# Top-p graph attention on one core: a 27-round search for the nucleus against a guess, two exact sums and 48 sorted candidates

## The chip, the cores and the metric

The kernel runs on one core of a Trainium2 chip. The core has five engines that run beside each other, each with its own queue of instructions that it takes strictly in order: TensorE (PE, with its weight loads PEld), VectorE (DVE), ScalarE (ACT), GpSimd (POOL) and SyncE (SP), which here only issues transfers. They wait for each other with semaphores. PE writes to PSUM; everything else lies in SBUF, 128 partitions wide. The metric is the device time of one execution in microseconds. All arithmetic is in float32.

## The reference

3,327 nodes with 256 features, an adjacency matrix `S` with about 0.12% of its entries set, and two steps of a graph layer. What matters:

```python
h = relu(layernorm(x))                         # X of what follows
def _top_p_attention(X, W1, W2, W3):
    q = X @ W1.T @ W2.T                        # 64 columns
    k = X @ W3.T
    probs = softmax(q @ k.T)                   # 3327 x 3327
    idx = argsort(-probs); sp = probs sorted
    keep_sorted = cumsum(sp) - sp < 0.9        # the nucleus of each row
    A = probs * mask
    return A / max(A.sum(-1), 1e-12)
R = (S + I) / rowsum
for n in range(2):
    A = _top_p_attention(Xa, W1, W2, W3)
    Xf = R @ Xf;  Xa = A @ Xa
    Z = Z + Xf @ U1[n].T + Xa @ U2[n].T
out = x + layernorm(X + Z) * g + b
```

Per row, the nucleus is the smallest set of the largest weights whose sum reaches 0.9 of the row's sum. Its size differs from row to row, and the reference finds it by sorting.

## The kernel before

The nodes are padded to 3,328 = 26 tiles of 128 rows. A tile's row of weights, 128 x 3,328, is a buffer `e`. Features (`x0`, `xf1`, `xa1`) and keys (`kT`) stay in SBUF for the whole run; only the adjacency, 1.7 MB per tile, comes from memory, once per step.

For each step the kernel first makes the keys of all tiles (L276), then works in groups of two tiles, 13 per step:

- `weights` (L124 to L145): queries, logits on PE in 512 columns each (L138), a copy from PSUM on ACT (L139), the row's maximum on DVE (L141), the exponential with its sum `z` on ACT (L143). It is called one group ahead.
- `diffuse` (L221 to L234): `R @ Xf` for the group's tiles on PE (L227), the input of the adjacency in two halves on SP.
- `nucleus` (L148 to L199): a binary search for the smallest weight of the nucleus, over the 27 low bits of a float, in place for both tiles of a group. Each round tries a candidate: ACT sums what lies over it (Relu, L165), DVE counts the weights that reach it (L168), and six DVE operations on two columns (L170 to L176, L162) turn the bit. After the rounds DVE zeroes what is smaller (L187), and treats weights equal to the threshold, of which only some belong to the nucleus, by a running count (L190, L192, L198, L199).
- `attend` (L202 to L216): transposes of `e` on PE (L208), copies of four at a time on ACT (L210), and `A @ Xa` on PE (L212), with the row's sum as column 257, whose reciprocal `ra` (L215) scales the result (L216).
- `finish` (L242 to L265), in the second step: the products with U1 and U2 (L253), a layernorm (L107 to L110, L261) and the output.

A scheduler orders each engine's instructions by their dependencies, so that a queue mixes instructions of neighbouring tiles: the work of attend and diffuse on PE and ACT lies beside the rounds of the next group. PE, with 30% of the span, waits most of the time.

In the listings, a name with a number is a buffer (`e_13582` is one tile's weights), and "waits" names the engine whose semaphore an instruction waits for.

## Time and profile before

| | |
|---|---|
| median of three runs | 7589.15 us (7588.61 to 7589.69) |
| profiled execution, span | 7591.1 us |
| instructions | 32,413 |
| busy: DVE, ACT, PE, POOL | 94%, 67%, 30%, 2% |
| transferred | 102.37 MB, mean 13 GB/s |

The profile is one execution; its own time is given by its span of 7591.1 us, the first to the last instruction, which is 2 us above the median of the runs. A row of a group reads: line, engine, operation, output<-inputs, size of the output and the input, count | total busy us, mean ns of one | idle time of the engine just before them and what ended it. A row of the timeline reads: start us, duration us, engine, line, operation. Matmuls come in float32 as two instructions for each matrix product of the code, so a tile's 26 blocks are 52 rows.

### The profile page before, as it was taken

The numbers are of one execution on the slowest core, as the hardware profiler recorded it, in microseconds if no ns is written. First come the engines' busy times: TensorE is split into PE (matmuls) and PEld (weight loads), VectorE is DVE, ScalarE is ACT, GpSimd is POOL, SyncE is SP. The second block draws the span as 40 slices with busy tenths as digits, with TensorE's granted clock in tenths as the row PEclk, the third lists the DMA queues.
The fourth block names the chain that finished last, engine by engine and source line by source line (L and its number), as shares of the span: only waits on it lengthen the run. The fifth ranks groups of instructions, "written<-read, shape, count | busy, mean of one in ns | idle before, by whom it ended". The sixth has DMA issues, their size and how long they took to land.

```text
span 7591.1 us, 32413 instructions
## 1 busy us (share of the span) xinstructions
PE 2264.7 (30%) x8840; PEld 1616.4 (21%) x8840; DVE 7155.3 (94%) x8060; ACT 5056.3 (67%) x4057; POOL 152.0 (2%) x295
## 2 busy tenths in 40 slices
PE   8783113113113113111324043043143142142222
PEld 5662102102102102101203032032032032132121
DVE  7999999999999999999789999999999999999997
ACT  6576676676676676676576766766766766766754
POOL 1000000000000000000000000000000000000000
PEclk9995555556556556555657576576576576576666
DMA  3230000000000000000000000000000000000000
GB/s 108 86 103 1 0 0 0 0 0 0 0 0 0 0 0 0 0 0 0 0 0 17 4 21 15 6 21 12 9 21 11 11 21 6 15 21 6 15 3 2
DMA packets 28071, 102.37 MB, mean 13 GB/s; under 512 B 3313, under 2 KB 14576, under 8 KB 27888
## 3 DMA queue, kind: packets, MB, share of 16 engines
q1 hardware_dynamic: 25888, 98.84, 4.0%
q10 hardware_dynamic: 2000, 1.46, 0.1%
q8 instruction: 70, 1.15, 0.1%
q14 instruction: 113, 0.93, 0.0%
HBM read 96.88 MB, written 3.41 MB: 13 GB/s over the span
## 4 chain that ended last, share of the span: by engine, by line
DVE 83%; ACT 7%; PE 6%; issue 4%; POOL 0%; DVEq 0%; DMA 0%; POOLq 0%; ACTq 0%
DVE jv L168 59%; ACT ja L165 5%; DVE nth L192 5%; PE pl L138 3%; DVE e L187 2%; DVE eq L198 2%; DVE e L199 2%; PE pr L227 2%; DVE low L172 2%; DVE cand L176 2%; DVE low L174 2%; DVE mass L171 1%; DVE ncand L162 1%; DVE mass L170 1%; ACT e L143 1%
## 5 line engine op out<-in xcount | busy, mean ns | idle before, releaser
L168 DVE TENSOR_SCALAR_CACHE_REDUCE jv<-e,cand 128x3328 uint8<-128x3328 f32 x1404 | 5161.3, 3676 | 36.6 <-ACT e L143 8.4
L165 ACT ACTIVATE ja<-e,ncand 128x3328 uint8<-128x3328 f32 x1404 | 4308.7, 3069 | 1197.8 <-DVE ncand L162 1173.3
L208 PE MATMUL pt<-ident,e 128*128 128x128 f32 x1352 | 208.9, 298 | 4770.2 <-DVE e L199 4770.2
L208 PEld LDWEIGHTS pt<-ident,e 128*128 128x128 f32 x1352 | 178.3, 154 | 4808.8 <-issue 4719.1
L210 ACT COPY eT<-pt 128x512 f32<-128x512 f32 (+1 forms) x364 | 189.5, 553 | 937.0 <-PE pt L208 936.7
L138 PE MATMUL pl<-kT,qT 64*128 64x512 f32 (+1 forms) x728 | 460.5, 778 | 77.3 <-ACT e L139 59.7
L212 PE MATMUL pa<-x,eT 128*128 128x257 f32 x1352 | 386.9, 446 | 152.7 <-ACT eT L210 82.5
L192 DVE TENSOR_TENSOR_SCAN nth<-eq 128x3328 int16<-128x3328 uint8 x52 | 368.6, 7088 | 0.9
L212 PE MATMUL pa<-xa,eT 128*128 128x257 f32 x1352 | 343.4, 407 | 47.5 <-ACT eT L210 47.5
L227 PE MATMUL pr<-x,at 128*128 128x257 f32 x1352 | 326.7, 400 | 77.3 <-issue 69.8
L227 PE MATMUL pr<-xf,at 128*128 128x256 f32 x1352 | 335.1, 396 | 29.3 <-DVE xf L233 25.0
L212 PEld LDWEIGHTS pa<-x,eT 128*128 128x128 f32 x1352 | 295.6, 226 | 225.0 <-ACT eT L210 101.2
L227 PEld LDWEIGHTS pr<-x,at 128*128 128x128 f32 x1352 | 265.9, 200 | 133.2 <-issue 83.7
L212 PEld LDWEIGHTS pa<-xa,eT 128*128 128x128 f32 x1352 | 266.5, 203 | 110.3 <-ACT eT L210 71.1
L227 PEld LDWEIGHTS pr<-xf,at 128*128 128x128 f32 x1352 | 256.4, 197 | 91.4 <-issue 31.6
L165 ACT ACTIVATION_READ_ACCUMULATOR ja<-e,ncand 128x1 f32 x1404 | 263.4, 188 | 0.0
L139 ACT COPY e<-pl 128x512 f32<-128x512 f32 (+1 forms) x364 | 188.0, 553 | 97.4 <-PE pl L138 97.4
L141 DVE TENSOR_REDUCE bias<-e 128x1 f32<-128x3327 f32 x52 | 187.9, 3613 | 52.9 <-ACT e L139 52.9
L138 PEld LDWEIGHTS pl<-kT,qT 64*128 64x128 f32 x728 | 161.1, 245 | 326.8 <-ACT e L139 201.9
L171 DVE TENSOR_TENSOR mass<-mass,over 128x2 f32<-128x2 f32 x702 | 113.6, 162 | 114.8 <-ACT ja L165 52.1
L198 DVE SCALAR_TENSOR_TENSOR eq<-nth,lim,eq 128x3328 uint8<-128x3328 int16 x52 | 191.8, 3689 | 1.8
L199 DVE SCALAR_TENSOR_TENSOR e<-eq,ncand,e 128x3328 f32<-128x3328 uint8 x52 | 191.6, 3685 | 1.9
(67 smaller groups left out, 2132.2 us busy)
## 6 DMA issues: line engine op xcount, KB each, us to landing
at<-in_adj SPq DMA_DIRECT2D x104, 832.0 KB, 4.4
xr<-in_x SPq DMA_DIRECT2D x26, 128.0 KB, 2.2
out<-y SPq DMA_DIRECT2D x25, 128.0 KB, 1.7
x<-in_x SPq DMA_DIRECT2D x6, 512.0 KB, 6.9
u<-in_u1t ACTq DMA_DIRECT2D x2, 256.0 KB, 5.7
u<-in_u2t ACTq DMA_DIRECT2D x2, 256.0 KB, 6.0
x<-in_x SPq DMA_DIRECT2D x1, 256.0 KB, 9.7
gam<-in_ln_g ACTq DMA_DIRECT2D x1, 128.0 KB, 5.1
```

What stands on the lines that cost most here:

```text
L138: nc.tensor.matmul(pl[:, :w], qT, kT[:, j : j + w], start=True, stop=True)
L139: nc.scalar.copy(e[:, j : j + w], pl[:, :w])
L165: nc.scalar.activation(ja, es[a], AF.Relu, bias=ncand[:, a : a + 1], accum_out=over[:, a : a + 1])
L168: nc.vector.tensor_scalar(jv, es[a], cand[:, a : a + 1], None, ALU.is_ge, ALU.add, accum_out=cnt[:, a : a + 1])
L171: nc.vector.tensor_tensor(mass, mass, over, ALU.add)
L192: nc.vector.tensor_tensor_scan(nth, eq, eq, 0.0, ALU.add, ALU.max)
L198: nc.vector.scalar_tensor_tensor(eq, nth, lim[:, c], eq, ALU.is_ge, ALU.mult)
L199: nc.vector.scalar_tensor_tensor(e, eq, ncand[:, c], e, ALU.mult, ALU.add)
L208: nc.tensor.transpose(pt[:, j, :], e[:, (j0 + j) * P : (j0 + j + 1) * P], ident)
L210: nc.scalar.copy(eT[:, :w, :], pt[:, :w, :])
L212: nc.tensor.matmul(pa, eT[:, j, :], xa[:, j0 + j, :], start=j0 + j == 0, stop=j0 + j == NT - 1)
L227: nc.tensor.matmul(pr[:, :w], at[:, j, :], xf[:, jj, :w], start=jj == 0, stop=jj == NT - 1)
```

## The change

The whole old layer stays, under the name `search_graph_layer`. A new `guess_graph_layer` does the layer with another search, and keeps a flag for every row whose answer cannot be vouched for. At the end PE adds up the flags, a register takes the sum, and a branch runs `search_graph_layer` as well if it is over zero.

The new search assumes that the logits of a row are roughly normal, so that weights are lognormal. The exponential is taken without the maximum, straight from PSUM (L477). From the row's sum and from the first two moments of its logits (which come out of one matmul with the mean and the second moments of the keys, `mq`) POOL computes by a fitted polynomial a threshold `c0` (column 9 of `g`), in about 27 operations on one column (`weights`). Then:

- `first`: ACT sums exactly what lies over `c0` (Relu, L520) and how many that are (Sign, L522). POOL makes a better threshold `c1` (column 13).
- `second`: DVE sums exactly what lies under `c1` (L536). POOL takes a secant step, adds a margin, and gets `c2` (column 16), meant to lie a little over the answer.
- `settle`: DVE zeroes everything from `c2` on (L571) and sums the rest; it finds the eight largest of each of 20 segments of 168 (L576), merges these 160 into the 48 largest in order (`ROUNDS` = 6, L581 and L583), adds them up from the largest down, compares with what is still needed, and zeroes in `e` what is smaller than the last candidate of the nucleus (L594). Its checks go to the flag (L599 to L605): that 48 were enough, that no segment had more than its eight, that no equal weights straddle the end, and that the sum lies in a range.
- `close`: `attend` as before, then `finish`, or in the first step `prep`, which makes the next step's keys, queries and moments. `spread` is the diffusion, with the adjacency in blocks of five tiles and three buffers.

The work goes tile by tile, not in groups, in a loop written in stages: in one turn settle of tile i, second of tile i+1, close of tile i-1, weights of tile i+3, first of tile i+2 and spread of tile i. Four buffers hold `e`. The keys lie in two halves of 64 partitions, so that two logit products of one turn stand on different rows of PE's array.

```diff
-        nucleus(es, z)
...
-            for i, t in enumerate(ts):
...
+        pq = ps_t.tile([P, 4, P], F32, tag="pt", name="pq")
+        PE.matmul(pq[:, 0, :], w2d[qp, :], qry[qp, j, :], start=True, stop=True)
+        PE.matmul(pq[:, 1:3, :].rearrange("p a b -> p (a b)")[:, : 2 * DA + 1], qry[qp, j, :],
+                  qm[qp, step, :], start=True, stop=True)
+        qT = tpool.tile([P, P], F32, tag="qT", name="qT", bufs=2)
+        S.copy(qT, pq[:, 0, :])
...
+        V.tensor_copy(mq[:, 0:1], pr_[:, 2 * DA : 2 * DA + 1])
+        qs = small.tile([P, DA], F32, tag="qs", name="qs", bufs=2)
+        V.tensor_copy(qs, pr_[:, :DA])
+        V.scalar_tensor_tensor(qj, qs, 1.0, pr_[:, DA : 2 * DA], ALU.mult, ALU.mult,
+                               accum_out=mq[:, 1:2])
+        G.memset(e[:, N:NP], 0.0)
...
+            if wd == 512:
+                S.activation(e.rearrange("p (a n) -> p a n", a=2)[:, :, c : c + wd], pl[:, :, :wd],
+                             AF.Exp, accum_out=za[:, n : n + 1])
...
+        G.tensor_tensor(g[:, 5:7], za[:, 0:2], za[:, 2:4], ALU.add)
+        G.tensor_tensor(col(0), col(5), col(6), ALU.add)
+        G.tensor_tensor(col(1), col(0), pwr[:, 5:6], ALU.pow)
+        G.tensor_scalar(col(1), col(1), 10.0, None, ALU.mult)
+        G.tensor_scalar(col(2), m, m, mq[:, 1:2], ALU.mult, ALU.subtract)
+        G.tensor_scalar(col(2), col(2), -1.0e-6, None, ALU.min)
+        G.tensor_scalar(col(3), col(2), -1.0, None, ALU.mult)
+        G.tensor_tensor(col(3), col(3), pwr[:, 3:4], ALU.pow)
+        G.tensor_scalar(col(5), col(2), -0.5, m, ALU.mult, ALU.add)
+        G.tensor_tensor(col(5), pwr[:, 1:2], col(5), ALU.pow)
+        G.tensor_scalar(col(5), col(5), col(0), 0.1 / N, ALU.mult, ALU.mult)
+        G.tensor_scalar(col(5), col(5), YLO, YHI, ALU.max, ALU.min)
+        G.tensor_tensor(col(4), col(5), pwr[:, 4:5], ALU.pow)
+        y = col(4)
+        G.tensor_scalar(col(6), y, PG[0], PG[1], ALU.mult, ALU.add)
+        for a in PG[2:]:
+            G.tensor_scalar(col(6), col(6), y, a, ALU.mult, ALU.add)
+        G.tensor_scalar(col(8), col(6), col(3), m, ALU.mult, ALU.add)
+        G.tensor_scalar(col(8), col(8), col(2), None, ALU.subtract)
+        G.tensor_tensor(col(9), pwr[:, 0:1], col(8), ALU.pow)
+        G.tensor_scalar(col(10), col(9), -1.0, None, ALU.mult)
+        G.tensor_scalar(col(7), y, -PK[0], -PK[1], ALU.mult, ALU.add)
+        G.tensor_scalar(col(7), col(7), y, -PK[2], ALU.mult, ALU.add)
+        G.tensor_scalar(col(11), col(7), col(3), None, ALU.mult)
...
+    def first(r):
+        e, col = r["e"], r["col"]
+        oa = small.tile([P, 2], F32, tag="oa", name="oa")
+        ja = scan.tile([P, NP], U8, tag="ja", name="ja")
+        S.activation(ja, e, AF.Relu, bias=col(10), accum_out=oa[:, 0:1])
+        ja = scan.tile([P, NP], U8, tag="ja", name="ja")
+        S.activation(ja, e, AF.Sign, bias=col(10), accum_out=oa[:, 1:2])
+        G.tensor_scalar(col(5), oa[:, 1:2], 0.5, NP / 2.0, ALU.mult, ALU.add)
+        G.tensor_scalar(col(5), col(5), col(9), oa[:, 0:1], ALU.mult, ALU.add)
+        G.tensor_scalar(col(5), col(5), col(0), col(1), ALU.subtract, ALU.mult)
+        G.tensor_scalar(col(12), col(5), -1.0, 0.1, ALU.mult, ALU.max)
+        G.tensor_scalar(col(5), col(12), 10.0, None, ALU.min)
+        G.tensor_tensor(col(5), col(5), col(11), ALU.pow)
+        G.tensor_scalar(col(13), col(5), col(9), None, ALU.mult)
+    def second(r):
+        e, col = r["e"], r["col"]
+        d1 = small.tile([P, 1], F32, tag="d1", name="d1")
+        jv = scan.tile([P, NP], F32, tag="w", name="jv")
+        V.scalar_tensor_tensor(jv, e, col(13), e, ALU.is_lt, ALU.mult, accum_out=d1)
+        r1, c1 = col(14), col(13)
+        G.tensor_scalar(r1, d1, col(1), 1.0e-6, ALU.mult, ALU.max)
...
+        G.tensor_tensor(col(6), col(6), col(5), ALU.pow)
+        G.tensor_scalar(col(6), col(6), c1, None, ALU.mult)
+        G.tensor_scalar(col(7), c1, 30.0, d1, ALU.mult, ALU.add)
+        G.tensor_scalar(col(7), col(7), col(0), BIG, ALU.is_gt, ALU.mult)
+        G.tensor_scalar(col(8), r1, 0.35, BIG, ALU.is_lt, ALU.mult)
+        G.tensor_scalar(col(16), col(6), col(7), col(8), ALU.add, ALU.add)
+    def settle(r, rows):
+        e, col = r["e"], r["col"]
+        d2 = small.tile([P, 1], F32, tag="d2", name="d2")
+        need = small.tile([P, 1], F32, tag="need", name="need")
+        w = scan.tile([P, NP], F32, tag="w", name="w")
+        V.scalar_tensor_tensor(w, e, col(16), e, ALU.is_lt, ALU.mult, accum_out=d2)
+        G.tensor_scalar(col(17), col(0), -0.1, None, ALU.mult)
+        G.tensor_tensor(need, d2, col(17), ALU.add)
+        cand = small.tile([P, NSEG * 8], F32, tag="cand", name="cand", bufs=1)
+        for s in range(NSEG):
+            V.max(cand[:, 8 * s : 8 * s + 8], w[:, s * SEG : min(NP, (s + 1) * SEG)])
+        v = small.tile([P, 4], F32, tag="v", name="v")
+        V.tensor_reduce(v[:, 0:1], cand.rearrange("p (s k) -> p s k", k=8)[:, :, 7], AX.X, ALU.max)
+        for k in range(ROUNDS):
+            b8 = bb[:, 1 + 8 * k : 9 + 8 * k]
+            V.max(b8, cand)
+            if k < ROUNDS - 1:
+                V.match_replace(cand, b8, cand, 0.0)
+        b = bb[:, 1 : TOPK + 1]
+        cum = small.tile([P, TOPK], F32, tag="cum", name="cum", bufs=1)
+        V.tensor_tensor_scan(cum, bb[:, :TOPK], bb[:, :TOPK], 0.0, ALU.add, ALU.max)
+        dr = small.tile([P, TOPK], F32, tag="dr", name="dr", bufs=2)
+        V.tensor_scalar(dr, cum, need, None, ALU.is_ge)
+        V.scalar_tensor_tensor(cum, dr, BIG, b, ALU.mult, ALU.add)
+        V.tensor_reduce(v[:, 1:2], cum, AX.X, ALU.min)
+        V.tensor_tensor(cum, dr, b, ALU.mult)
+        V.tensor_reduce(v[:, 2:3], cum, AX.X, ALU.max)
+        V.scalar_tensor_tensor(e, e, v[:, 1:2], e, ALU.is_ge, ALU.mult)
...
+        G.tensor_scalar(f, dr[:, TOPK - 1 : TOPK], 1.0, None, ALU.is_ge)
...
+        G.tensor_scalar(fl[n], f[n], 5.5, fl[n], ALU.is_lt, ALU.add)
...
+    for step in range(2):
+        moments(step)
+        for i in range(-3, NT + 1):
+            if 0 <= i < NT:
+                settle(live[step, i], rows_of(i))
+            if 0 <= i + 1 < NT:
+                second(live[step, i + 1])
+            if i >= 1:
+                close(step, i - 1)
+            if 0 <= i + 3 < NT:
+                live[step, i + 3] = weights(step, i + 3)
+            if 0 <= i + 2 < NT:
+                first(live[step, i + 2])
+            if 0 <= i < NT:
+                spread(step, i)
+    pf = ps_t.tile([P, 4, P], F32, tag="pt", name="pf")
+    PE.matmul(pf[:1, 0, :1], fl, ones, start=True, stop=True)
+    V.tensor_copy(flag, pf[:1, 0, :1])
...
+def tile_graph_layer(ctx, tc, *args):
+    keep = ctx.enter_context(tc.tile_pool(name="keep", bufs=1))
+    flag = keep.tile([1, 1], I32, tag="flag", name="flag")
+    guess_graph_layer(tc, *args, flag)
+    failed = tc.nc.values_load(flag[0:1, 0:1], min_val=0, max_val=1 << 20)
+    with tc.If(failed > 0):
+        search_graph_layer(tc, *args)
```

In the listings that follow, tile A has the buffer `e_13582` and tile A+1 `e_13900`, both in the middle of the second step. First DVE before, at the end of a group's search: rounds (L168 to L176) and the passes behind them.

```order
L168 TENSOR_SCALAR jv_6973,cnt_6601<-e_5737,cand_6598 128x3328
L168 TENSOR_SCALAR jv_6977,cnt_6601<-e_5778,cand_6598 128x3328 [waits DVE_49]
L170 TENSOR_TENSOR mass_6602<-cand_6598,cnt_6601 128x2 [waits DVE_49]
L171 TENSOR_TENSOR mass_6602<-mass_6602,over_6600 128x2 [waits DVE_49,Activation_49]
L172 TENSOR_TENSOR low_6603<-mass_6602,thr_6597 128x2 [waits DVE_49]
L174 TENSOR_SCALAR low_6603<-low_6603 128x2 [waits DVE_49]
L176 TENSOR_TENSOR cand_6598<-cand_6598,low_6603 128x2 [waits DVE_49]
L181 RECIPROCAL rc_6984<-cand_6598 128x2 [waits DVE_49]
L182 TENSOR_SCALAR ncand_6599<-cand_6598 128x2
L187 SCALAR_TENSOR_TENSOR e_5737,mass_6602<-e_5737,cand_6598 128x3328
```

The rounds follow each other, and each needs only the last.

DVE after, from the end of settle of tile A to the start of settle of tile A+1:

```order
L594 SCALAR_TENSOR_TENSOR e_13582<-e_13582,v_14346 128x3328 [waits Activation_49]
L651 TENSOR_TENSOR y_13873<-pz_13844,x0_95 128x256 [waits DMAHW1_49,PE_49,Activation_49]
L459 COPY mq_13894<-pq_13889 128x1 [waits Activation_49]
L461 COPY qs_13897<-pq_13889 128x64
L402 BN_STATS st_13878<-y_13873 128x6 [waits DVE_49]
L462 SCALAR_TENSOR_TENSOR qj_13895,mq_13894<-qs_13897,pq_13889 128x64 [waits DVE_49]
L403 BN_AGGR mv_13879<-st_13878 128x2 [waits DVE_49]
L593 TENSOR_REDUCE v_14346<-cum_14359 128x1
L656 TENSOR_SCALAR y_13873<-y_13873,mv_13879,rstd_13880 128x256 [waits DVE_49,Pool_49]
L638 TENSOR_TENSOR xf2_13959<-pr_13960,xf1_96 128x256 [waits PE_49]
L536 SCALAR_TENSOR_TENSOR jv_14377,d1_14376<-e_13900,g_13922 128x3328 [waits Activation_49,Pool_49]
L571 SCALAR_TENSOR_TENSOR w_14639,d2_14637<-e_13900,g_13922 128x3328 [waits DVE_49,Pool_49]
```

The pass L536 of `second` and the pass L571 of `settle`, both of tile A+1, stand next to each other, with nothing between; `mq` of tile A+1 stands behind L594 of tile A.

ACT before: the Relu of the rounds, with the copies of attend between them.

```order
L165 ACTIVATE ja_12875,over_12854<-e_11907,ncand_12853 128x3328 [waits DVE_49]
L119 COPY xT_12550<-pt_12547 128x256 [waits PE_49]
L210 COPY eT_12584<-pt_12579 128x512 [waits PE_49,Activation_49]
L165 ACTIVATE ja_12879,over_12854<-e_11948,ncand_12853 128x3328 [waits Activation_49]
L210 COPY eT_12595<-pt_12590 128x512 [waits PE_49]
L210 COPY eT_12606<-pt_12601 128x512 [waits PE_49]
L165 ACTIVATE ja_12889,over_12854<-e_11907,ncand_12853 128x3328 [waits DVE_49,Activation_49]
```

ACT after: the exponentials of tile A+1 (L477 to L482), then its Relu and Sign, then the copies of attend of an earlier tile.

```order
L454 COPY qT_13892<-pq_13889 128x128 [waits PE_49]
L477 ACTIVATE e_13900,za_13901<-pl_13903 128x2x512 [waits PE_49]
L477 ACTIVATE e_13900,za_13901<-pl_13907 128x2x512 [waits PE_49]
L477 ACTIVATE e_13900,za_13901<-pl_13911 128x2x512 [waits PE_49]
L481 ACTIVATE e_13900,zb_13918<-pl_13915 128x128 [waits PE_49]
L482 ACTIVATE e_13900,za_13901<-pl_13915 128x127
L520 ACTIVATE ja_14266,oa_14265<-e_13900,g_13922 128x3328 [waits Activation_49,Pool_49]
L522 ACTIVATE ja_14268,oa_14265<-e_13900,g_13922 128x3328 [waits Activation_49]
L616 COPY eT_14091<-pt_14086 128x512 [waits PE_49]
```

The two sums of tile A+1 now come directly after its exponentials, and the copies of attend stand behind them.

POOL after, where before it had only the few operations of layernorm and diffusion: the end of `weights` of tile A+1 (L508), its `first` (L523 to L529), and the start of its `second` (L538).

```order
L508 TENSOR_SCALAR g_13922<-g_13922 128x1 [waits Pool_49]
L523 TENSOR_SCALAR g_13922<-oa_14265 128x1 [waits Activation_49]
L524 TENSOR_SCALAR g_13922<-g_13922,oa_14265 128x1 [waits Pool_49]
L525 TENSOR_SCALAR g_13922<-g_13922 128x1 [waits Pool_49]
L639 TENSOR_SCALAR xf2_13959<-xf2_13959,rrs_101 128x256 [waits DVE_49]
L526 TENSOR_SCALAR g_13922<-g_13922 128x1 [waits Pool_49]
L527 TENSOR_SCALAR g_13922<-g_13922 128x1 [waits Pool_49]
L541 TENSOR_SCALAR g_13922<-g_13922 128x1
L528 TENSOR_TENSOR g_13922<-g_13922 128x1 [waits Pool_49]
L529 TENSOR_SCALAR g_13922<-g_13922 128x1 [waits Pool_49]
L552 TENSOR_SCALAR g_13922<-g_13922 128x1 [waits Pool_49]
L538 TENSOR_SCALAR g_13922<-d1_14376,g_13922 128x1 [waits DVE_49]
```

Three stages of one tile stand in one queue behind each other; L523 waits for ACT's sums and L538 for DVE's `d1`.

More of the change, by code (lines that the diff above doesn't have):

```diff
@@ L38, in tile_graph_layer, with search_graph_layer @@
 @with_exitstack
-def tile_graph_layer(
+def search_graph_layer(
     ctx: ExitStack,
@@ L307 @@
+@with_exitstack
+def tile_graph_layer(ctx, tc, *args):
[5 more added lines that the diff above has]
+        search_graph_layer(tc, *args)
 def kernel(x, adj, L0_gnn_W1, L0_gnn_W2, L0_gnn_W3, L0_gnn_U1, L0_gnn_U2, L0_gnn_ln_g, L0_gnn_ln_b):
```

241 lines of the change are left out of this document (added).

## The prediction

> **What bounds the kernel now.** First the page's own lines: span, busy time by engine, granted clock, the chain of waits, and the two costliest groups.
>
> ```profile
> span 7591.1 us, 32413 instructions
> PE 2264.7 (30%) x8840; PEld 1616.4 (21%) x8840; DVE 7155.3 (94%) x8060; ACT 5056.3 (67%) x4057; POOL 152.0 (2%) x295
> DVE 83%; ACT 7%; PE 6%; issue 4%; POOL 0%; DVEq 0%; DMA 0%; POOLq 0%; ACTq 0%
> L168 DVE TENSOR_SCALAR_CACHE_REDUCE jv<-e,cand 128x3328 uint8<-128x3328 f32 x1404 | 5161.3, 3676 | 36.6 <-ACT e L143 8.4
> L165 ACT ACTIVATE ja<-e,ncand 128x3328 uint8<-128x3328 f32 x1404 | 4308.7, 3069 | 1197.8 <-DVE ncand L162 1173.3
> ```
>
> DVE is busy 94% of the span and on 83% of the chain: the search is the kernel. The timeline of DVE shows one round, and with it the prices of small operations.
>
> ```profile
> 63.03 3.68 DVE L168 TENSOR_SCALAR_CACHE_REDUCE jv<-e,cand 128x3328 uint8<-128x3328 f32 x1 [4.22 <-ACT e L143]
> ...
> 5000.71 3.67 DVE L168 TENSOR_SCALAR_CACHE_REDUCE jv<-e,cand 128x3328 uint8<-128x3328 f32 x1
> ...
> 5004.30 0.08 DVE L168 DVE_READ_ACCUMULATOR jv<-e,cand 128x1 f32 x1
> ...
> 5008.60 0.16 DVE L172 TENSOR_TENSOR low<-mass,thr 128x2 int32<-128x2 f32 x1
> 5008.80 0.17 DVE L174 TENSOR_SCALAR low<-low 128x2 int32<-128x2 int32 x1
> ...
> 5009.28 3.67 DVE L168 TENSOR_SCALAR_CACHE_REDUCE jv<-e,cand 128x3328 uint8<-128x3328 f32 x1
> ...
> 5017.45 0.43 DVE L107 BATCH_NORM_STATS2 st<-y 128x6 f32<-128x256 f32 x1
> 5017.92 0.18 DVE L108 BATCH_NORM_AGGREGATE mv<-st 128x2 f32<-128x6 f32 x1
> ```
>
> A round of two tiles is 8.57 us (5000.71 to 5009.28), 27 of them 231 us, and there are 26 such groups: 6,020 of 7,591 us. A DVE operation that needs the one before starts 0.20 us after it on 2 columns (5008.60 to 5008.80) and 0.47 on 256 (5017.45 to 5017.92).
>
> **The other prices.** The groups by line, then POOL and PE in the timeline of the last two tiles, where nothing else runs beside them.
>
> ```profile
> L192 DVE TENSOR_TENSOR_SCAN nth<-eq 128x3328 int16<-128x3328 uint8 x52 | 368.6, 7088 | 0.9
> L187 DVE SCALAR_TENSOR_TENSOR e<-e,cand 128x3328 f32<-128x3328 f32 x52 | 189.4, 3680 | 0.0
> L141 DVE TENSOR_REDUCE bias<-e 128x1 f32<-128x3327 f32 x52 | 187.9, 3613 | 52.9 <-ACT e L139 52.9
> L165 ACT ACTIVATION_READ_ACCUMULATOR ja<-e,ncand 128x1 f32 x1404 | 263.4, 188 | 0.0
> L210 ACT COPY eT<-pt 128x512 f32<-128x512 f32 (+1 forms) x364 | 189.5, 553 | 937.0 <-PE pt L208 936.7
> L234 POOL TENSOR_SCALAR xf<-xf,rrs 128x256 f32<-128x256 f32 x52 | 48.4, 930 | 3374.5 <-DVE cand L176 2585.4 <-DVE mass L170 361.5 <-DVE rrs L232 321.5
> L259 POOL TENSOR_TENSOR xr<-xr,bet 128x256 f32<-128x256 f32 x26 | 19.0, 731 | 67.2 <-DMA xr<-in_x 67.2
> ```
> ```profile
> 7559.00 0.23 POOL L109 TENSOR_SCALAR rstd<-mv 128x1 f32<-128x1 f32 x1 [225.38 <-DVE mv L108]
> 7559.32 0.57 POOL L110 TENSOR_TENSOR rstd<-rstd,mhalf 128x1 f32<-128x1 f32 x1
> 7559.92 0.41 DVE L261 TENSOR_SCALAR y<-y,mv,rstd 128x256 f32<-128x256 f32 x1 [1.01 <-POOL rstd L110]
> ...
> 7563.85 3.75 PE L212 MATMUL pa<-xa,eT 128*128 128x257 f32 x16 [0.30 <-ACT eT L210]
> 7568.76 3.75 PE L212 MATMUL pa<-xa,eT 128*128 128x257 f32 x16 [0.29 <-ACT eT L210]
> ```
>
> POOL is free now, 2%. A one-column operation on it, with the next one needing it, takes 0.30 us (7559.00 to 7559.32, rounded down) and a power 0.65 (0.57 and the step of 0.08 to the next). L234 against L259 says that a scalar read through a pointer can cost 0.2 more on 256 columns; on one column I take 0.08.
>
> **The change, part by part.** Removed: 27 rounds, the scan L192, two passes (L190, L198), the max L141. Added per tile on DVE: three passes of L187's kind (L536, L571, L594), 20 MAX over 168, six MAX and five MATCH_REPLACE over 160, five operations on 48; on ACT a Relu and a Sign; on POOL about 75 one-column operations. By busy time alone that would be some 24 us a tile, where DVE's 7,155 us over 52 tiles are 138 now. But every step's result feeds the next, and the order of instructions decides what overlaps. From about the sixth tile of a step on, DVE holds second(A+1) (L536) and directly behind it w(A+1) (L571) of the same tile; between them lie the 22 POOL operations of `second`. While DVE waits there, nothing behind it can start. POOL does weights(A+1) after mq(A+1), which stands on DVE behind e(A) (L594); ACT's Relu and Sign (A+1) wait for that; `first` waits for them; second(A+1) for that. So a tile is a ring without overlap, and I add it up.
>
> DVE's share: three passes of 3.76 (L187's 3.68 and a read of 0.08) are 11.3. A MAX: 168 elements at L141's 1.09 ns are 0.18, at the scan's 2.13 ns 0.36, with 0.06 fixed 0.24 to 0.42; I take 0.26, since it is one reading pass like L141: 20 are 5.2. Eleven MAX and MATCH_REPLACE over 160, each needing the last, are 0.47 less 96 columns of 1 ns, 0.37: 4.1. The reduce 0.25, five 48-wide at 0.23 1.15. ra, mq, qs, qj and the small adds for diffusion 1.5. Together 23.5 in the first step, 23.9 in the second with y and its statistics.
>
> ACT's share: Relu and Sign at 3.07 + 0.19 each, 6.5; in the first step two copies of 0.55 stand between them and add 1.2: 7.7.
>
> POOL's share, first step: 57 operations, 8 of them powers: 49 × 0.30 + 8 × 0.65 = 19.9; 24 pointers × 0.08 add 1.9. Second step: 66 operations, with 256-wide ones at 0.73 (rstd, gam, xr and bet stand before weights in its queue), 24.8; 30 pointers add 2.4. Six changes of engine at 0.1 are 0.6.
>
> The ring: 23.5 + 7.7 + 19.9 + 1.9 + 0.6 = 53.6, taken 53.5, and 23.9 + 6.5 + 24.8 + 2.4 + 0.6 = 58.2, taken 58.5. In the first five or six tiles of a step the queues still hold the stages of three tiles mixed, so POOL's chain and DVE's share overlap in part; I take 32 and 37 (POOL's share plus half of DVE's rest), an estimate.
>
> What hides under the ring: PE, and the copies of attend. The prices of a matmul come from stretch 50:550, where PE is dense.
>
> ```profile
> L227 PE MATMUL pr<-x,at 128*128 128x257 f32 x1330 | 319.0, 400 | 73.5 <-issue 69.8 <-PE pr L227 3.7
> L138 PE MATMUL pl<-kT,qT 64*128 64x512 f32 (+1 forms) x82 | 36.9, 583 | 0.6 <-ACT e L139 0.5
> L212 PE MATMUL pa<-x,eT 128*128 128x257 f32 x104 | 26.3, 408 | 5.0 <-ACT xa L216 5.0
> L208 PE MATMUL pt<-ident,e 128*128 128x128 f32 x52 | 7.3, 275 | 2.5 <-DVE e L199 2.5
> ```
> ```profile
> 100.00:200.00 100.00, 80.20 (x350) 67.40 (x348) 96.38 (x132) 74.00 (x47) 5.55 (x6) 0.97 0.36 115
> 500.00:600.00 100.00, 55.78 (x231) 46.62 (x229) 96.73 (x124) 73.45 (x47) 3.70 (x4) 0.80 0.26 86
> 5000.00:5500.00 500.00, 124.21 (x500) 86.86 (x498) 477.30 (x555) 357.30 (x279) 12.09 (x22) 0.63 0.04 14
> ```
>
> Per tile 52 × 0.240 + 52 × 0.253 + 26 × 0.14 + 14 × 0.45 + 2.2 = 37.8 us, and 41 with finish. The table by stretch (PE busy, PEld, DVE, ACT, POOL, clock, DMA share, GB/s) shows the granted clock at 0.97 where PE is 80% busy, 0.80 at 56%, 0.63 at 25%. After the change PE does the same matmuls in a third of the time: 38 of 53.5 is 71%, so about 0.9, and PE stays below the ring. The input of adj in blocks of 5 tiles is 1.7 MB in 53 us, 32 GB/s, where 115 stands above: hidden. The table of exponentials read without the maximum removes L141 and puts nothing on DVE. The flag, its matmul and the branch: some 10 us once.
>
> The sum: prelude (first search starts at 63 now; the keys' second product and the moments added, an estimate) 85, the first tile's own way through the stages 61, 5 × 32 = 160, 20 × 53.5 = 1,070, and 50 for the last two attends with prep (8 of the 26 blocks take 4.91 us, 7563.85 to 7568.76, so one attend 16 and its ends 5 to 9); second step 62 + 5 × 37 = 247, 20 × 58.5 = 1,170, attend and finish 58, end 12: 2,913, taken 2,900. It is made against the profiled execution, 7,591 us of span; the runs' median is 7,589.15, 0.03% less, which I neglect.
>
> **Two rules weighed.** The pl row is 0.45 us for each of 14, one after another.
>
> The Trainium skill, "TensorE: Matmul & The Clock Gate", section "Packing small matmuls — row/col tiling", says that matmuls on different rows of the array run at the same time; the keys now lie in two halves of 64 partitions, so by it the 14 would cost 3.2 us a tile and not 6.3. No run here shows it; the sum would fall by at most 1.7 us a tile in the first step, about 45 us, as most of that is hidden.
>
> The Trainium skill, "SBUF — State Buffer", section "SBUF: two separate sides", says that a DVE instruction with two inputs from SBUF and a GpSimd one that reads SBUF exclude each other for the whole instruction; this speaks against the change, as L594 has two inputs while POOL has chains to run. None of the rows above has both at once; by it the sum would grow by 35 to 75 us, an estimate.
>
> **The rivals.** *The engines overlap* (0.13): if the ring is looser than I read it, PE is next: (37.8 + 41) × 26 + 85 + 110 = 2,245, and 2,100 to 2,500. For it: PE could work through the waits. Against: the queues are in order and DVE stands at L571.
>
> *POOL is dearer* (0.15): if a pointer operation costs 0.45 to 0.5 and not 0.38, 54 of them over both rings at 0.12, and powers with other exponents 1.0 and not 0.65, 8 × 0.35, add 5 to 10 us a tile: 46 × 7 = 320, so 3,200 to 3,500. For it: L234's 0.93 against 0.73, and only one exponent (−0.5) is on show.
>
> *The clock does not rise* (0.06): if it stayed at 0.63 as in 5000:5500, PE's 38 to 41 at 0.95 become 57 to 62, over the ring: 3,250. Against: the stretch 100:200.
>
> *The branch is taken* (0.045): one row of 6,654 whose answer is not among its 48 candidates raises the flag, and the whole old search runs behind the new one: 2,900 + 7,580 = 10,480, slower. Carrying the guess through for the reference's inputs in single precision leaves no row over; the deepest needs place 45 of 48, and the nearest pair of neighbours lies 1.0038 apart, so errors of 0.1% in the exponentials would do it. That is also how the change would not do what it says.
>
> **How the numbers follow.** The ring as summed has 0.615, the rivals 0.13, 0.15, 0.06 and 0.045. Predicted 2,900. The range: below, MAX at 0.24, pointers at nothing and half the handoffs give 46 × 3 = 140 less, and a shorter first part 100 less: 2,650 within the ring; some of the overlap case brings it to 2,400. Above, MAX at 0.42 adds 3.2 a tile (150) and the dear POOL most of the rest: 3,400. Left out are the branch, most of the overlap case, and the tail of the dear POOL, together about 2 in 10. Within 0.2% (15 us) is what a measurement can't tell from no change; no case lands there: 0.005. Faster 0.95, slower 0.045.
>
> **What would show it.** Right: DVE idle before L571 by 7 to 9 us and before L536 by 20 to 27, released by POOL; POOL's chain the largest part of the chain of waits; periods of e L594 near 53 and 58 with the clock at 0.85 to 0.95. Wrong: PE busy above 90% (overlap), POOL one-column rows above 0.35 (dear POOL), MAX rows at 0.40, L168 present at all (the branch), PE clock below 0.7 with DVE waiting for attend. The page's POOL share should go from 2% to some 40%.

## The result and the profile after

The changed kernel takes 3012.05 us (median of four runs, 3011.24 to 3014.73) where the kernel before takes 7589.42 us: a ratio of 0.3969, 95% interval 0.3964 to 0.3975. The forecast was 2,900 (2,400 to 3,400), 4% below. The branch to the old search was not taken: L168 is absent.

The page of the kernel after, in the parts that were shown of before: span, busy time by engine, and the chain of waits by engine and by line.

```profile
span 3010.9 us, 28189 instructions
PE 2023.4 (67%) x9055; PEld 1557.0 (52%) x9055; DVE 1188.7 (39%) x3075; ACT 841.3 (28%) x1536; POOL 1538.8 (51%) x3711
...
POOL 43%; PE 18%; DVE 16%; ACT 11%; issue 10%; DMA 2%; SPq 0%; ACTq 0%; POOLq 0%; DVEq 0%
PE pr L632 6%; DVE w L571 6%; POOL g L552 6%; ACT ja L522 5%; DVE cand L576 4%; PE pz L648 4%; ACT ja L520 4%; POOL f L600 3%; PE pa L618 2%; DVE cand L583 2%; DVE bb L581 2%; DMA xr<-in_x 1%; POOL g L504 1%; PE pk L423 1%; PE pt L412 1%
```

No engine is full. DVE fell from 7,155 to 1,189 us of work, and POOL, from 2% to 51%, carries the largest part of the chain. The groups of DVE and POOL by line (busy us, mean ns of one | idle time ahead of it and who ended it) show where the queues stand still.

```profile
L536 DVE SCALAR_TENSOR_TENSOR jv<-e,g 128x3328 f32<-128x3328 f32 x52 | 191.7, 3686 | 754.4 <-POOL g L529 754.4
L571 DVE SCALAR_TENSOR_TENSOR w<-e,g 128x3328 f32<-128x3328 f32 x52 | 192.2, 3697 | 435.1 <-POOL g L563 412.3 <-POOL e L466 16.3 <-POOL kr L431 6.5
L576 DVE MAX8 cand<-w 128x8 f32<-128x168 f32 (+1 forms) x1040 | 253.6, 317 | 1.1
L552 POOL TENSOR_SCALAR g<-g 128x1 f32<-128x1 f32 x52 | 180.7, 3476 | 5.3
L600 POOL TENSOR_SCALAR f<-v,f 128x1 f32<-128x1 f32 x52 | 172.0, 3308 | 16.0 <-DVE v L591 15.3
```

DVE waits 754 us for POOL's `first` (L529) and 435 us for POOL's `second` (412 of them for L563), together 40% of the span: the two waits that the prediction named. Two rows stand out: L552 and L600 are one-column operations like their neighbours, and yet take 3.5 and 3.3 us each.

One turn of the ring, from the timeline of DVE, POOL and ACT in the middle of the second step (start, duration, operation, and in brackets the idle time ahead of it):

```profile
2100.02 3.69 DVE L536 SCALAR_TENSOR_TENSOR jv<-e,g 128x3328 f32<-128x3328 f32 x1 [12.23 <-POOL g L529]
2111.87 3.69 DVE L571 SCALAR_TENSOR_TENSOR w<-e,g 128x3328 f32<-128x3328 f32 x1 [8.16 <-POOL g L563]
2126.02 3.68 DVE L594 SCALAR_TENSOR_TENSOR e<-e,v 128x3328 f32<-128x3328 f32 x1
2144.54 0.42 DVE L638 TENSOR_TENSOR xf<-pr,xf 128x256 f32<-128x256 f32 x1 [10.90 <-PE pr L632]
2158.77 3.69 DVE L536 SCALAR_TENSOR_TENSOR jv<-e,g 128x3328 f32<-128x3328 f32 x1 [13.81 <-POOL g L529]
```
```profile
2126.04 3.83 POOL L600 TENSOR_SCALAR f<-v,f 128x1 f32<-128x1 f32 x1 [0.34 <-DVE v L591]
2131.49 0.38 POOL L492 TENSOR_SCALAR g<-mq 128x1 f32<-128x1 f32 x1 [1.62 <-DVE mv L403]
2140.34 0.72 POOL L654 TENSOR_TENSOR xr<-xr,bet 128x256 f32<-128x256 f32 x1 [2.69 <-DMA xr<-in_x]
2141.29 0.19 POOL L488 TENSOR_TENSOR g<-za 128x2 f32<-128x2 f32 x1
2155.77 0.19 POOL L523 TENSOR_SCALAR g<-oa 128x1 f32<-128x1 f32 x1 [5.55 <-ACT ja L522]
```
```profile
2149.33 3.07 ACT L520 ACTIVATE ja<-e,g 128x3328 uint8<-128x3328 f32 x1 [14.04 <-POOL g L508]
```

From one L536 to the next it is 58.75 us, and the pieces follow each other: the pass and its read 3.8, second on POOL 8.1, L571 3.7, MAX and rounds 10.5 (to 2126.02), L594 and the small operations 5.5, flag, layernorm and the wait for `xr` on POOL 9.8 (to 2141.29), weights 8.0 (to 2149.33), Relu and Sign 6.4, first 3.0.

### The profile page after: what moved, and what is told of

Same layout as the page of the kernel before. It is cut to its first block, busy times and chain, and to the rows that moved or that the text cites. A ratio compares the mean times of both kernels' runs of the same rounds, so it can differ in the third digit from the quotient of the medians.

```text
span 3010.9 us, 28189 instructions
## 1 busy us (share of the span) xinstructions
PE 2023.4 (67%) x9055; PEld 1557.0 (52%) x9055; DVE 1188.7 (39%) x3075; ACT 841.3 (28%) x1536; POOL 1538.8 (51%) x3711
## 4 chain that ended last, share of the span: by engine, by line
POOL 43%; PE 18%; DVE 16%; ACT 11%; issue 10%; DMA 2%; SPq 0%; ACTq 0%; POOLq 0%; DVEq 0%
PE pr L632 6%; DVE w L571 6%; POOL g L552 6%; ACT ja L522 5%; DVE cand L576 4%; PE pz L648 4%; ACT ja L520 4%; POOL f L600 3%; PE pa L618 2%; DVE cand L583 2%; DVE bb L581 2%; DMA xr<-in_x 1%; POOL g L504 1%; PE pk L423 1%; PE pt L412 1%
## 5 line engine op out<-in xcount | busy, mean ns | idle before, releaser
L536 DVE SCALAR_TENSOR_TENSOR jv<-e,g 128x3328 f32<-128x3328 f32 x52 | 191.7, 3686 | 754.4 <-POOL g L529 754.4
L616 ACT COPY eT<-pt 128x512 f32<-128x512 f32 (+1 forms) x364 | 186.2, 554 | 647.1 <-PE pt L614 646.9
L571 DVE SCALAR_TENSOR_TENSOR w<-e,g 128x3328 f32<-128x3328 f32 x52 | 192.2, 3697 | 435.1 <-POOL g L563 412.3
L520 ACT ACTIVATE ja<-e,g 128x3328 uint8<-128x3328 f32 x52 | 159.5, 3067 | 703.9 <-POOL g L508 703.9
L576 DVE MAX8 cand<-w 128x8 f32<-128x168 f32 (+1 forms) x1040 | 253.6, 317 | 1.1
L648 PE MATMUL pz<-u,xT 128*128 128x256 f32 x416 | 143.1, 506 | 149.2 <-ACT xa L622 148.8
L473 PE MATMUL pl<-k,qT 64*128 64x512 f32 (+1 forms) x832 | 196.4, 589 | 66.8 <-ACT e L477 62.2
L594 DVE SCALAR_TENSOR_TENSOR e<-e,v 128x3328 f32<-128x3328 f32 x52 | 191.7, 3687 | 0.0
L477 ACT ACTIVATE e<-pl 128x1024 f32<-128x1024 f32 x156 | 158.6, 1020 | 98.3 <-PE pl L473 98.1
L552 POOL TENSOR_SCALAR g<-g 128x1 f32<-128x1 f32 x52 | 180.7, 3476 | 5.3
L600 POOL TENSOR_SCALAR f<-v,f 128x1 f32<-128x1 f32 x52 | 172.0, 3308 | 16.0 <-DVE v L591 15.3
```

Source lines behind the costliest of these rows:

```text
L473: PE.matmul(pl[:, a, :wd], qT[p, :], keys[step][p].rearrange("p a b -> p (a b)")[:, c : c + wd], start=True, stop=True)
L520: S.activation(ja, e, AF.Relu, bias=col(10), accum_out=oa[:, 0:1])
L536: V.scalar_tensor_tensor(jv, e, col(13), e, ALU.is_lt, ALU.mult, accum_out=d1)
L552: G.tensor_scalar(col(7), c1, col(1), 14.0, ALU.mult, ALU.mult)
L571: V.scalar_tensor_tensor(w, e, col(16), e, ALU.is_lt, ALU.mult, accum_out=d2)
L576: V.max(cand[:, 8 * s : 8 * s + 8], w[:, s * SEG : min(NP, (s + 1) * SEG)])
```

## Experiments

The ring theory says: each tile's stages stand one behind another because of the order in the queues, not because an engine is full. Its rivals: PE and its clock, POOL's total, or the number of buffers. Times below are medians; each run's ratio is to the kernel before on the same chip, and differences are taken to the 3012 of the kernel after.

### Eight operations more on POOL

```diff
         G.tensor_scalar(r1, d1, col(1), 1.0e-6, ALU.mult, ALU.max)
+        for _ in range(8):
+            G.tensor_scalar(r1, r1, 1.0, None, ALU.mult)
```

> Eight more one-column operations on POOL in second, each needing the last, multiplying by one. In a ring each of them is on the path: a dependent one starts 0.35 to 0.40 us after the one before, 8 x 0.37 x 46 to 52 tiles = 136 to 154, so 3,140 to 3,175. If PE or DVE's total is the limit and POOL's chain runs beside it, 3,010 to 3,030.

Measured: 3077.85 us, ratio 0.4057 (0.4050 to 0.4064): 66 more. The lines of this kernel are two higher than in the kernel after.

```profile
L573 DVE SCALAR_TENSOR_TENSOR w<-e,g 128x3328 f32<-128x3328 f32 x52 | 191.8, 3688 | 543.7 <-POOL g L565 454.4 <-POOL e L466 73.5 <-POOL kr L431 15.8
```

POOL is on the path: in steady tiles of both steps L536 to L571 is now 14.2 us and not 11.85, 2.3 us for eight operations, or 0.29 each where 0.37 had been costed. L573's wait grew by 109 us (435.1 to 543.7), but the time only by 66. In the first step the period rose by some 2 us, from 52 to 54. In the second step it rose by 2 only where POOL's queue kept its order. In about half of its steady tiles the scheduler put the operation that waits for `xr` behind the first operations of weights, and the wait shrank to between 0 and 2.1 us:

```profile
L656 POOL TENSOR_TENSOR xr<-xr,bet 128x256 f32<-128x256 f32 x26 | 18.8, 722 | 41.0 <-DMA xr<-in_x 40.9
```

In the kernel after this row (L654 there) waits 63.9 us. So 23 us were won back by another order, which the edit brought with it; what is still missing is not accounted for.

### Second on DVE

```diff
-        G.tensor_scalar(col(5), col(12), r1, None, ALU.subtract)
+        V.tensor_scalar(col(5), col(12), r1, None, ALU.subtract)
...
-        G.tensor_tensor(col(5), col(5), pwr[:, 5:6], ALU.pow)
+        V.reciprocal(col(5), col(5))
```

The other operations of `second` likewise; the last power stays on POOL.

> The kernel after, with the one-column operations of second on DVE, where a dependent one takes 0.20 us and not 0.36, but for the last power, which stays on POOL; the two other powers become reciprocals. The stretch from L536 to L571 shrinks from 8.1 us to about 5.2. If that stretch is on the ring in every tile: 3 x 46 = 140 less, 2,870. If, as the eight operations more showed (66 for 150), the path over ACT's copies and PE's attend ends at about the same time, a third to a half of it: 2,940 to 2,970. If neither: 3,012.

Measured: 2622.90 us, ratio 0.3457 (0.3451 to 0.3463): 389 less, more than any theory had. The timeline of DVE in this run, from L594 of one tile to L571 of the next, and POOL's operations from L492 on:

```profile
2093.96 3.69 DVE L594 SCALAR_TENSOR_TENSOR e<-e,v 128x3328 f32<-128x3328 f32 x1
...
2122.69 3.68 DVE L536 SCALAR_TENSOR_TENSOR jv<-e,g 128x3328 f32<-128x3328 f32 x1 [1.20 <-POOL g L529]
2130.72 3.69 DVE L571 SCALAR_TENSOR_TENSOR w<-e,g 128x3328 f32<-128x3328 f32 x1
```
```profile
2093.79 0.42 POOL L492 TENSOR_SCALAR g<-mq 128x1 f32<-128x1 f32 x1 [0.17 <-DVE qj L462]
2104.37 0.19 POOL L488 TENSOR_TENSOR g<-za 128x2 f32<-128x2 f32 x1
2112.44 0.73 POOL L654 TENSOR_TENSOR xr<-xr,bet 128x256 f32<-128x256 f32 x1
```

L536 to L571 is 8.0 us where it was 11.85: 3.8 less, where 2.9 had been expected. The rest is order: in this run the scheduler put `mq` ahead of L594 and the operation that waits for `xr` (L654) behind the chain of weights, so that from L594 to L488 it is 10.4 us (2093.96 to 2104.37) and no longer 15.3. Together 8.7 a tile in the second step, whose period fell from 59.5 to 51; and in the first step the loose stretch, with periods of 23 to 40 us, lasted until about the 13th tile, not the sixth. No run has the one without the other.

### No second read of x

```diff
-        nc.sync.dma_start(xr, x[t * P : (t + 1) * P])
-        G.tensor_tensor(xr, xr, bet, ALU.add)
+        G.tensor_tensor(xr, bet, bet, ALU.add)
```

> The kernel after without the second read of x in finish (the output lacks that x). In the kernel after POOL waits 2.7 us a tile for this transfer in the second step, ahead of the chain of weights, and only after it has read the old xr does the transfer start. If POOL's queue is the ring there, 20 to 22 tiles lose 2.7 us: 55 to 60 less, 2,950 to 2,957. If the wait runs beside the path over PE, less than 20.

Measured: 2972.58 us, ratio 0.3914 (0.3908 to 0.3921): 39 less, where 55 to 60 had been expected. The period of the second step fell from 59.5 to between 55.5 and 58. A wait of POOL for one transfer is paid in full only until the next path is as long: in most of the later tiles `y` (L651) starts 5.2 us after the start of L594, when PE's products of finish are done, and not 3.6, when the pass is.

### A pass with one input

```diff
-        V.scalar_tensor_tensor(e, e, v[:, 1:2], e, ALU.is_ge, ALU.mult)
+        V.tensor_scalar(e, e, v[:, 1:2], None, ALU.is_ge, ALU.add, accum_out=v[:, 3:4])
...
-    with tc.If(failed > 0):
+    with tc.If(failed > 1000000):
```

> L594 is a pass of the same length with one input from SBUF (it writes 0 or 1 where the kernel multiplies by the weight, so the rows of weights are a mask; the branch never runs). If L600 takes 3.3 us because a DVE pass with two inputs keeps POOL from reading, L600 falls to 0.3 us, L552 (beside L536, which keeps its two inputs) stays at 3.5, and the flag's operations run under the pass: 1 to 2.5 us a tile on some 46 tiles, 2,900 to 2,965. If L600 is slow for another reason (the first operation after a wait, the kind of operand), it stays at 3.3 us and the time at 3,012.

Measured: 2989.12 us, ratio 0.3938 (0.3932 to 0.3945): 23 less, half of the least that had been expected (47 to 112). The groups of DVE and POOL in this run:

```profile
L594 DVE TENSOR_SCALAR_CACHE_REDUCE e<-e,v 128x3328 f32<-128x3328 f32 x52 | 190.9, 3672 | 0.0
```
```profile
L600 POOL TENSOR_SCALAR f<-v,f 128x1 f32<-128x1 f32 x52 | 20.1, 386 | 16.5 <-DVE v L591 16.0
L601 POOL TENSOR_SCALAR f<-v,f 128x1 f32<-128x1 f32 x52 | 19.3, 371 | 131.0 <-DVE v L593 68.9 <-DVE qj L462 47.3 <-DVE ra L621 7.3
L552 POOL TENSOR_SCALAR g<-g 128x1 f32<-128x1 f32 x52 | 170.6, 3282 | 5.3
```

The pass is as long as before (3672 ns), and L600 fell from 3,308 to 386 ns, while L552, beside a pass that kept its two inputs, stayed at 3.3 us. So a pass with a second input from SBUF keeps POOL out until it ends, and one of the same length with a single input does not (the operation of the pass is another one, too). The Trainium skill, "SBUF — State Buffer", section "SBUF: two separate sides", states that a VectorE instruction with two SBUF inputs and a GpSimd one that reads SBUF exclude each other. This run agrees (3,308 against 386 ns). But the price is small: behind L600, the next flag operation L601 needs `v` from L593, which stands on DVE behind L594 anyway, and L552 is followed by L538, which needs the result of the pass. The block mostly takes the place of a wait.

### The queues in written order

```diff
-        for i in range(-3, NT + 1):
+        with tc.manual_schedule(engines={mybir.EngineType.DVE, mybir.EngineType.Pool}):
+          for i in range(-3, NT + 1):
```

> The same instructions; DVE and POOL issue them in the order in which the loop of stages is written (settle i, second i+1, close i-1, weights i+3, first i+2, spread i), where the scheduler had put second and settle of one tile side by side. If the ring through the queues is what takes 52 and 59 us a tile, weights, first and second of later tiles now run on POOL and ACT while DVE settles, L571 waits only for the rest of second's POOL chain, and the tile falls to what PE needs, 38 to 41 us: 26 x 79 + ends of 250 = 2,300 (2,200 to 2,500). If PE with its clock, or POOL's total, is the limit whatever the order, the time stays at 2,950 to 3,050.

Measured: 2597.20 us, ratio 0.3424 (0.3418 to 0.3430): 415 less, with the same instructions. So the order is shown to be what makes most of the ring; but 2,300 was expected. The page's engines of the chain, and ACT's timeline:

```profile
PE 50%; POOL 26%; ACT 15%; issue 6%; DVE 2%; DMA 1%; POOLq 0%; SPq 0%; ACTq 0%; DVEq 0%
```
```profile
933.10 3.07 ACT L520 ACTIVATE ja<-e,g 128x3328 uint8<-128x3328 f32 x1 [10.02 <-POOL g L508]
936.07 0.19 ACT L520 ACTIVATION_READ_ACCUMULATOR ja<-e,g 128x1 f32 x1
936.29 3.07 ACT L522 ACTIVATE ja<-e,g 128x3328 uint8<-128x3328 f32 x1
939.26 0.19 ACT L522 ACTIVATION_READ_ACCUMULATOR ja<-e,g 128x1 f32 x1
939.36 1.05 ACT L616 COPY eT<-pt 128x512 f32<-128x512 f32 x2
```

A second ring of 44.4 and 47.8 us a tile appeared: the copies of attend (L616) stand on ACT behind a Relu that waits 10 us for POOL. With ACT in written order too:

> As the run with DVE and POOL in written order, and ACT in written order too. In that run the copies of attend stood on ACT behind Relu and Sign of a later tile, which wait for POOL's chain, so PE's attend, the next logits, the exponentials, POOL and ACT followed each other in a ring of 44 and 48 us. If that is what holds it, the copies now stand ahead of Relu, PE runs through, and a tile takes PE's 38 to 41 at a clock of 0.9, 40 to 43: 26 x 83 + 270 = 2,430 (2,300 to 2,480). If POOL is the limit by itself (31 us busy a tile and some 12 in which DVE's passes keep it out), the time stays at 2,560 to 2,600.

Measured: 2371.38 us, ratio 0.3126 (0.3121 to 0.3131). The copies now run while POOL is busy, the period is 42 and 40.3 us, as expected.

```profile
PE 1925.9 (81%) x9055; PEld 1490.8 (63%) x9055; DVE 1205.4 (51%) x3075; ACT 839.4 (35%) x1536; POOL 1614.6 (68%) x3711
...
POOL 66%; PE 14%; issue 12%; DVE 3%; ACT 3%; DMA 1%; POOLq 0%; ACTq 0%; DVEq 0%
...
L601 POOL TENSOR_SCALAR f<-v,f 128x1 f32<-128x1 f32 x52 | 363.1, 6982 | 5.7
```

PE is 81% busy, and POOL's queue is the chain. With PE in written order as well:

> As order_act, with PE in written order too: the products of the diffusion no longer stand between transposes and products of attend, and each of seven groups waits for its copy. If PE is the limit by then, seven waits of about 1 us are added to each tile: 52 x 7 = 360 more than order_act, 2,650 to 2,850. If something else is, less than 100 more.

Measured: 2885.30 us (one run), with periods of 51 to 52 us: 514 more than with ACT, where 7 a tile had been expected and 10 to 11 came. The expectation's reason, that the scheduler's products of diffusion between those of attend fill the waits for the copies, is not tested apart: the run fixes all of PE's order.

### Three buffers

```diff
-    epool = ctx.enter_context(tc.tile_pool(name="e", bufs=4))
+    epool = ctx.enter_context(tc.tile_pool(name="e", bufs=3))
```

> Three buffers for e and not four, with the scheduler's order. With three the scheduler puts attend of a tile directly behind its settle, and mq of tile A+2 between second and settle of A+1, so that weights of A+2 can start while A+1 settles. If the order in the queues is what makes the ring, the time falls although there is a buffer less: 2,600 to 2,900. If the number of tiles in flight is what limits, it rises: 3,100 to 3,400.

Measured: 2903.83 us, ratio 0.3826 (0.3820 to 0.3833): 108 less with a buffer less. Its order on DVE, L594 of tile A, then L536 of A+1, then `mq` of A+2, then L571 of A+1, gives periods of 51 and 54.5. The number of tiles in flight is not the limit. With four buffers the scheduler lets attend fall behind: in steady tiles of the second step it ends some 175 us after L594 of its tile, three periods; with three buffers it is 115, two periods. So the fourth buffer holds a finished tile. More than half of the 108 us comes at the ends of the steps, where fewer tiles wait for attend: from the last L594 of the first step to the first of the second it is 133 us and not 172, and behind the last one 85 and not 109.

### What is left in the best order

Three runs build on the one with DVE, POOL and ACT in written order (2371.38).

> The run with DVE, POOL and ACT in written order, and L594 again as a pass of the same length with one input (rows of weights become a mask; the branch never runs). In that run POOL was on 66% of the chain of waits, and its L601 took 6.98 us, the length of L594 and L536, which follow each other with two inputs each. If DVE's passes keep POOL out, L601 falls to about 3.5 us, and as POOL sets the end, 3.5 us a tile come off where PE leaves room: 42 and 40.3 fall to 38 to 40, 100 to 180 less, 2,190 to 2,270. If the blocking hides work that would wait anyway, less than 40.

Measured: 2317.32 us, ratio 0.3052 (0.3047 to 0.3057): 54 less, half of the least that had been expected. Periods fell from 42 to 41 and from 40.3 to 38.3 or 39.7. The block is gone from L601, but a shorter one appears at the next ready operation (L498, 1.6 us mean), beside another pass:

```profile
L498 POOL TENSOR_SCALAR g<-g 128x1 f32<-128x1 f32 x52 | 82.0, 1576 | 5.9
```

> DVE, POOL and ACT in written order, and second's one-column operations on DVE (the last power stays on POOL). POOL loses some 8 us a tile, DVE gains 4.4 on 24 and stays free for a third. If POOL with its blocking is what holds the run with the three orders, PE is the limit now, at 37 to 39 us a tile with a clock of 0.95: 2,150 to 2,250. If it is PE already, 2,350 to 2,371.

Measured: 2386.09 us, ratio 0.3143 (0.3138 to 0.3149), 15 more or 0.6%: this expectation failed. The first step fell to 40 us a tile, but the second rose to 44. There POOL now stands still at L404, the first operation of finish's layernorm. First the row in this run, then in the one with the three orders:

```profile
L404 POOL TENSOR_SCALAR rstd<-mv 128x1 f32<-128x1 f32 x52 | 11.7, 226 | 265.2 <-DVE mv L403 260.2 <-ACT x L667 3.4
L404 POOL TENSOR_SCALAR rstd<-mv 128x1 f32<-128x1 f32 x52 | 11.2, 215 | 36.7 <-DVE mv L403 30.1 <-ACT x L667 2.8
```

The moved operations stand on DVE ahead of `ra`, on which attend's end, PE's finish and `y` (L651) hang. In one turn `ra` comes 8.6 us after the start of L536 (1731.64 to 1740.22) where it was 3.6 (1726.42 to 1730.03), and POOL, which used to do second in that time, has nothing to do until `y` and its statistics are there: 9.3 to 9.9 us a tile, then all of weights. The first step has no finish, so it keeps the gain. That is read from the traces; no run moves `ra` alone.

```diff
             if 0 <= i < NT:
                 spread(step, i)
+                vouch(live[step, i], rows_of(i))
```

`vouch` holds the flag's operations (L599 to L605), which stood at the end of `settle`.

> The run with DVE, POOL and ACT in written order, with the flag's seven operations moved on POOL from behind settle to the end of the loop's turn, so that none of them stands ready while L594 and L536 run, and second's chain follows L536 at once. In the run with the three orders the one operation kept out (L601, 6.98 us) was 15% of the chain of waits. If that block delays the chain of second: 2 to 4 us a tile less where PE leaves room (41.9 and 40.3 to about 39), 2,230 to 2,310. If POOL's total is the limit and another operation is kept out in its place: 2,350 to 2,375.

Measured: 2444.48 us, ratio 0.3221 (0.3217 to 0.3225): 73 more, wrong in sign. L601's block is gone (358 ns for the same operation, now L604); another operation, L495, is kept out in its place, 1,908 ns in the mean where 567 was seen. And the seven operations now stand on POOL ahead of `need` (L573), for which DVE's L589 waits. In this run:

```profile
L589 DVE TENSOR_SCALAR dr<-cum,need 128x48 f32<-128x48 f32 x52 | 12.9, 248 | 325.2 <-POOL need L573 324.8
```

With the flag in its place, in the run with the three orders, the wait was a quarter less:

```profile
L589 DVE TENSOR_SCALAR dr<-cum,need 128x48 f32<-128x48 f32 x52 | 12.9, 247 | 244.5 <-POOL need L573 244.1
```

So 2371.38 us is the fastest of the kernels here that do the whole computation, 21% less than the kernel after.

### The price of the branch

```diff
-    G.memset(fl, 0.0)
+    G.memset(fl, 1.0)
```

> The flag starts at one in every row, so that the branch is taken: the new search's 3,012 and the whole old one's 7,589 behind it, 10,590 to 10,620; L168 is there with 1404 rows. If the second part gains from what lies loaded already, up to 20 less.

Measured: 10606.58 us (one run). By stretch, the new search and behind it the old one:

```profile
0.00:3020.00 3020.00, 2018.26 (x9055) 1553.85 (x9055) 1190.05 (x3086) 842.11 (x1536) 1546.27 (x3716) 0.83 0.12 35
3020.00:10604.00 7584.00, 2271.81 (x8840) 1618.03 (x8840) 7151.57 (x8051) 5055.65 (x4056) 151.32 (x286) 0.63 0.04 13
```

The cut at 3,020 us is a round one: the old search's first transfers are issued from 3,008 on. From there it is 7,597 us to the end, so the second part is the kernel before, unshortened. One row out of 6,654 costs 7.6 ms. What a branch that is not taken costs was not measured, since every kernel with the new search has it.

## Why the prediction was right

**The ring.** Predicted 53.5 and 58.5 us a tile, measured (steady tiles, start of L594 to the next) 52 and 59.5. The mechanism is the forecast one: POOL's chain is the largest part of the chain of waits, DVE idles 8.2 us before L571, and the queues in another order take the ring apart. By parts, in the turn of the second step shown above: DVE 23.9 predicted, 23.5 measured; ACT 6.5 and 6.4; POOL 27.2 and 28.9. A MAX takes 0.244 us (253.6 / 1,040), the low end of the bounds, where 0.26 was taken. One-column operations kept to 0.30 to 0.40 from start to start, so the dear POOL did not come. The sign for L536 was half missed: its wait is 14.5 us in the mean (754.4 / 52) and not 20 to 27. In the second step L638's wait of 10.9 us for PE takes up the rest of the same gap.

The prediction missed POOL's wait of 2.7 us for `xr`, since it costed that transfer at nothing, and it put `mq` behind L594 in both steps alike. In the first step `mq` is copied ahead of L594, which takes operations off the ring, and the ring closes over POOL's flag operations instead. The chain of waits there reads (start, duration, operation):

```profile
924.45 3.83 POOL f L600
929.05 0.57 POOL g L490
...
935.63 0.58 POOL g L507
936.56 3.17 ACT ja L520 x2
```

Against that, DVE waits there for PE's `prep` in the middle of its rounds, which the prediction had hidden under the ring, up to 2.9 us a tile:

```profile
970.31 0.22 DVE L435 TENSOR_TENSOR gsum<-gsum,pg 64x65 f32<-64x65 f32 x1 [2.66 <-PE pg L434]
```

So the 52 us of the first step lie near the 53.5 partly by luck: two errors of the reading take each other back.

**The second path.** That PE and attend hide under the ring was right for their sum, but not with room to spare. From `ra` among the rounds of DVE a second path runs over ACT, PE's products of finish or prep and back to DVE. In the second step `y` starts 3.6 to 5.3 us after the start of L594, and 3.6 is the pass alone, so PE ends up to 1.7 us after it. In the first step it is L435's wait.

**The ends.** This is the term that was mis-sized, and it is more than the whole difference:

| part, us | predicted | measured |
|---|---|---|
| to the first L594 | 146 | 202 |
| 25 periods of the first step | 1,230 | 1,194 |
| last L594 to the next step's first | 112 | 172 |
| 25 periods of the second step | 1,355 | 1,333 |
| after the last L594 | 70 | 109 |

The rings are 58 us shorter than predicted, the ends 155 longer; that the time came within 4% owes something to these opposite signs. About 62 of the 155 lie in the first tile's own way through the stages: 91 us and not 61 in the first step (from the last key at 111), 93 and not 62 in the second (from 1,475). The queues are the reason here, too. L594 of the first tile stands on DVE behind L571 of the next, which waits for POOL:

```profile
195.29 3.68 DVE L571 SCALAR_TENSOR_TENSOR w<-e,g 128x3328 f32<-128x3328 f32 x1 [13.29 <-POOL g L563]
```

Most of the rest is attend. At a step's end three tiles wait for it, not two, and each comes with its diffusion. The stretches behind the last L594 of either step show PE alone at work, full, at the whole clock:

```profile
1400.00:1477.00 77.00, 77.00 (x399) 64.36 (x399) 3.90 (x19) 14.34 (x35) 5.58 (x13) 1.00 0.20 61
2905.00:2992.00 87.00, 84.57 (x427) 71.52 (x426) 6.43 (x19) 14.57 (x32) 13.92 (x24) 1.00 0.18 53
```

At some 27 us a tile, three tiles are 77 us where 50 had been put down for two with prep; at the end it is 109 and not 70. The keys at the start, 26 tiles at 3.3 us, took until 111, where the estimate was 85.

**The clock.** Predicted 0.85 to 0.95; the rows of the two steps show less, with PE 65 and 67% busy.

```profile
700.00:1100.00 400.00, 260.03 (x1132) 198.22 (x1133) 171.22 (x451) 117.56 (x210) 204.89 (x504) 0.79 0.09 26
2200.00:2600.00 400.00, 267.90 (x1154) 207.08 (x1155) 154.55 (x391) 104.31 (x176) 201.53 (x479) 0.83 0.11 33
```

What that cost is not shown, as no run changes the clock alone; PE is 18% of the chain of waits. In the run with three queues in written order PE is 81% busy, and the mean clock is 0.895 where it is 0.826 here.

**The two rules.** The products of queries and keys by group:

```profile
L473 PE MATMUL pl<-k,qT 64*128 64x512 f32 (+1 forms) x832 | 196.4, 589 | 66.8 <-ACT e L477 62.2 <-ACT qT L454 4.5
```

They are 196.4 / 52 = 3.8 us a tile, where 6.3 had been put down from the kernel before. That agrees with the Trainium skill, "TensorE: Matmul & The Clock Gate", section "Packing small matmuls — row/col tiling", by whose rule the prediction's estimate was 3.2. What this was worth in time no run shows. The second rule, on DVE's second input, is shown by L552 and L600; its price was put at 35 to 75 us and measured as 23 for L594, one of the two passes that keep an operation out in each tile.

**The rivals.** No branch; no dear POOL; a clock well above 0.63; the engines do not overlap by themselves, but can: 2371 us is inside what that rival gave (2,100 to 2,500).

## What to carry to other kernels

When a long serial search is replaced by many short stages on several engines, add up one turn of the queues in the order in which they stand, not the busy times; DVE's busy time said 24 us a tile, the queues 52 to 60. A stage whose result the next instruction of the same queue needs overlaps with nothing in that queue: the same instructions in another order took 21% less. Count the first tile and the last ones by the queues as well; here the ends held most of the error. And before an operation is moved, look for what already waits at that place: a block of 3 us that lies under another wait is worth tenths of it, and a moved operation can stand ahead of something that mattered. A small edit can also give the scheduler another order, so read the order again before a difference is put down to the edit.

## What the runs showed of the hardware

- A POOL operation on one column takes 3.3 to 3.8 us and not 0.3 if it comes up while DVE runs a pass over 3,328 elements with two inputs in SBUF, and 7.0 us when two such passes follow each other. With one input of the same pass it takes 0.39.
- The eight largest of 168 take DVE 0.244 us from start to start; MATCH_REPLACE over 160 0.31 us.
- Products over 512 columns that alternate between two halves of 64 partitions take 0.28 us each of PE's busy time (176.1 / 624, kernel after), where 0.49 was seen with all in one half (34.0 / 70, kernel before, 50 to 550 us).
